# Moving the end of a scan chunk off VectorE, six convolution pairs to TensorE, and a looser queue in layer 0

## The chip, the cores and the metric

The kernel runs on one core of one Trainium2 chip, in one launch. The metric is the device time of that launch in microseconds (us), the median of several runs. Five engines work side by side, each through its own queue in order: TensorE (PE; its weight loads are PEld), VectorE (DVE), ScalarE (ACT), GpSimd (POOL) and SyncE (SP), which here issues only DMA transfers. They meet through semaphores. PE writes its results to PSUM tiles, which DVE and ACT read; the other tiles lie in SBUF.

## What is computed

Two layers on x of shape 4 x 256 x 512 (1024 tokens in 8 blocks of 128), each with a residual.

Layer 0 is an attention with 32 heads over latents of width 4, followed by a gated feed-forward of hidden width 1792:

```python
C_q = x @ Wq_d + bq_d ; C_kv = x @ Wkv_d + bkv_d
q = (C_q @ W_qk + b_qk).reshape(b, s, 32, 4)
attn = softmax(einsum('bqhd,bkd->bhqk', q, C_kv) / sqrt(4))
x = x + (attn over C_kv @ Wv_u + bv_u) @ Wo + bo + down(silu(gate(x)) * up(x))
```

Layer 1 is a selective-scan block (1024 channels, 16 states, a causal convolution of 4 taps) beside a feed-forward with a router that picks two of eight low-rank experts:

```python
x, z = split(hidden @ in_proj_w)
xc = silu(conv_b + sum over k of conv_w[:, k] * x shifted by 3 - k)
dt, Bm, Cm = rmsnorm'd parts of xc @ x_proj_w ; dt = softplus(dt @ dt_proj_w + dt_bias)
h_t = exp(dt_t * A) * h_(t-1) + dt_t * B_t * x_t        # for 1024 x 16 states, 256 steps
y = (sum over n of h * C + D * xc) * silu(z)
out = y @ out_proj_w
```

The four batches of 256 tokens are independent in the scan.

## The kernel before

**Layer 0** lets PE work without a break. The feed-forward is written as a generator, `gate_up` and then `down`, that issues a few matmuls at each step; `go(ff, n)` takes n steps of it. The attention's pieces are issued between such steps, so that PE has feed-forward matmuls in its queue while other engines finish the attention's evictions. Weights of gate and up (`wgu`, 256 KB each) are fetched by POOL's queue three tiles ahead.

Each batch first needs its latents (`latents`, L284 to L338, a generator as well, taken one `yield` at a time). It projects the keys and queries, copies them out of PSUM, and splits them into a rounded high part (ACT) and the rest as a low part (DVE's subtraction: `ks` on L296, `q` low on L320). L310 multiplies q out, DVE adds its bias and scales it (L314, twice), and four spread matmuls give `qg`, whose evictions on L337 alternate between DVE and ACT. `scores_max` (L352, L354) then has PE write scores into PSUM and DVE take their maxima, 64 reductions in all; PE reuses the two score banks once DVE is through with them. Two passes of `maxima` and `attention` cover the four batches. Before layer 1, SP loads the in-projection's weights `w_in`, 512 KB for a pair of chunks (L621): the first as soon as the pool is open, the second and third inside the loop over the last normalization (L633 to L636).

**Layer 1's scan** is a loop over u = 0 to 127 (4 batches x 8 chunks of 128 channels x 4 groups of four states). A step is, in this order of the queues: ACT computes four decays for step u + 2 (L958, 128 x 255 each); DVE multiplies `bx` (L964, 128 x 1024, into PSUM) from `brow` and `dus`; DVE runs the scan (L979); POOL multiplies the states by C into `hc` (L984); PE sums hc over the states into the PSUM tile `ysum` (L996, one step later). There are two h tiles, three hc tiles and one ysum. When the four steps of a chunk are through, `close_chunk` (L1000), issued two steps after the chunk's last, multiplies ysum with silu(z) and writes the chunk's result: on DVE, between bx and the scan. The next chunk's first matmul into ysum (L994) follows it.

All other work of a batch (the next batch's normalization, in-projection, convolution, step sizes dt, and the last batch's output and experts) is put into the loop by a table written out by hand: `put(b, s, f, ...)` runs f at step s of batch b, ahead of bx, and `put_late` at its end. `dt` and `du = dt * x` of a pair of chunks are stored to DRAM by SP (`send`) and read back in the scan's layout, `dts` and `dus` (`spread`, four transfers of 32 partitions each, two tiles deep). For batch 0 the table holds later steps than for the others, because its second half has to be made while its first half is scanned: `step_out` (three POOL operations that finish dt) and `step_x` (POOL's du).

The convolution takes two chunks, a pair, at a time: `conv_in` at one step and `conv_taps` at the next. From batch 1 on, the pair's first chunk is convolved by PE with four diagonal matrices that ACT scales (L767, L789) and evicted by ACT (L791); the second chunk is four scaled copies on ACT (L768 and L772) that POOL adds up (L795, three adds of 128 x 256).

## Time and profile before

The median of three runs is 850.35 us (850.3 to 854.58). One execution was profiled:

| | |
|---|---|
| profiled execution, whole | 852.26 us |
| its span in the trace | 850.5 us |
| mean granted clock of PE | 0.954 |
| busy: PE, DVE, ACT, POOL | 740.6, 669.6, 538.6, 489.1 us |
| DVE scan, L979 | 129 times, 2234 ns each |
| DVE bx, L964 | 128 times, 1232 ns |
| POOL hc, L984 | 130 times, 2322 ns |
| ACT decays, L958 | 504 times, 498 ns |
| DVE closing multiply, L1000 | 32 times, 416 ns, after 9.7 us of idle |
| POOL convolution adds, L795 | 45 times, 729 ns |

How to read it. A line of the timeline is: start, duration, engine, source line, operation, the tile written and those read, shapes, how many were joined; in brackets how long the engine had been idle before, and what ended that idle time. A line of the waits gives the same summed over the execution: engine and tile, what it waited for, and total us, times and the longest. The busy table says how long each engine worked, but not whether anybody waited for it; the granted clock says at what share of full speed PE was let run in a stretch.

### The profile page before, as it was taken

How to read it: one execution, taken by the hardware profiler on the slowest of the kernel's cores; microseconds unless marked ns; L12 is line 12 of the kernel's file. 1: busy time of each engine (PE TensorE's matmuls, PEld its weight loads, DVE VectorE, ACT ScalarE, POOL GpSimd, SP SyncE). 2: the span in 40 equal slices, each digit the busy share in tenths (PEclk: the TensorE clock that was granted, in tenths of full speed). 3: DMA queues.
4: the chain of work that ended last, by engine and by line, in shares of the span. 5: the costliest groups of instructions: out<-in, count | busy, mean ns of one | idle time of the engine just before them, and what ended most of it. 6: DMA issues, size and time to landing. Idle time of an engine off the chain costs nothing.

```text
span 850.5 us, 10982 instructions
## 1 busy us (share of the span) xinstructions
PE 740.6 (87%) x3798; PEld 423.6 (50%) x3798; DVE 669.6 (79%) x647; ACT 538.6 (63%) x1061; POOL 489.1 (58%) x376
## 2 busy tenths in 40 slices
PE   5999999989999899989778888887898997956875
PEld 3565546656555676656444346344356444312331
DVE  4597755478744435798799999899999999999996
ACT  4225565223566267599885789786888885855561
POOL 3223322001343333669967689869599759697664
PEclk9999999899999999999898999989999979998998
DMA  7234332001222322555751644433553343443400
GB/s 223 68 94 125 88 86 62 0 1 38 75 75 79 113 56 63 139 147 161 206 142 50 173 137 124 123 100 109 156 155 99 102 112 102 109 119 105 112 25 25
DMA packets 67202, 86.71 MB, mean 102 GB/s; under 512 B 12061, under 2 KB 52009, under 8 KB 66762
## 3 DMA queue, kind: packets, MB, share of 16 engines
q1 hardware_dynamic: 57786, 67.12, 28.5%
q0 software_dynamic: 9072, 18.35, 7.8%
q8 instruction: 30, 0.49, 0.2%
q10 hardware_dynamic: 288, 0.52, 0.2%
q14 instruction: 26, 0.21, 0.1%
HBM read 66.58 MB, written 10.22 MB: 90 GB/s over the span
## 4 chain that ended last, share of the span: by engine, by line
PE 37%; DVE 30%; POOL 12%; ACT 8%; issue 6%; DMA 4%; SPq 1%; DVEq 0%; POOLq 0%; ACTq 0%
DVE h L979 18%; POOL hc L984 7%; PE pu L444 6%; PE pg L444 6%; DVE bx L964 6%; ACT decay L958 4%; PE av L397 4%; PE po L469 3%; PE scT L386 2%; DVE mpl L354 2%; PE px L753 2%; POOL xc L795 2%; PE pz L926 2%; DMA dus<-dud 2%; PE ysum L996 1%
## 5 line engine op out<-in xcount | busy, mean ns | idle before, releaser
L984 POOL TENSOR_TENSOR hc<-h,cr 128x1024 f32<-128x1024 f32 (+1 forms) x130 | 301.6, 2322 | 96.4 <-DVE h L979 76.6
L979 DVE TENSOR_TENSOR_SCAN h<-decay,bx 128x1024 f32<-128x1024 f32 (+1 forms) x129 | 288.0, 2234 | 16.3 <-PE po L469 4.0
L958 ACT ACTIVATE decay<-dts,aneg 128x255 f32<-128x255 f32 x504 | 213.3, 498 | 97.5 <-DVE h L979 87.2
L964 DVE TENSOR_TENSOR bx<-brow,dus 128x1024 f32<-128x1024 f32 x128 | 157.7, 1232 | 8.7 <-DMA dus<-dud 4.6
L996 PE MATMUL ysum<-hc,stack 128*32 128x256 f32 x1024 | 88.1, 413 | 60.1 <-POOL hc L984 59.8
L456 POOL TENSOR_TENSOR hlo<-g,hhi 128x512 fp32r<-128x512 f32 x28 | 35.9, 1281 | 118.3 <-ACT hhi L455 118.3
L427 POOL DMA_DIRECT2D wgu<-in_wgu x56 | 31.2, 558 | 97.3 <-PE pg L444 95.9
L354 DVE TENSOR_REDUCE mpl<-sc 128x4 f32<-128x1024 f32 x64 | 76.4, 1217 | 12.4 <-PE sc L352 12.2
L996 PEld LDWEIGHTS ysum<-hc,stack 128*32 128x32 f32 x1024 | 21.2, 111 | 120.7 <-POOL hc L984 98.1
L388 ACT ACTIVATE pe<-scT 128x1024 f32<-128x1024 f32 x64 | 64.0, 1023 | 23.4 <-PE sc L352 16.8
L1088 PE MATMUL po<-ow,xc 128*128 128x512 f32 x128 | 70.4, 659 | 2.2 <-DVE xc L1000 2.2
L926 PE MATMUL pz<-xn1T,w_in 128*128 128x256 f32 x256 | 67.5, 411 | 0.0
L753 PE MATMUL px<-xn1T,w_in 128*128 128x256 f32 x256 | 61.8, 387 | 0.1
L926 PEld LDWEIGHTS pz<-xn1T,w_in 128*128 128x128 f32 x256 | 49.0, 200 | 19.0 <-issue 10.8
L753 PEld LDWEIGHTS px<-xn1T,w_in 128*128 128x128 f32 x256 | 48.2, 192 | 13.1 <-issue 4.3
L452 DVE SCALAR_TENSOR_TENSOR g<-g,pg 128x512 f32<-128x512 f32 x28 | 19.2, 686 | 41.5 <-ACT g L451 41.5
L444 PE MATMUL pu<-xhi,wgu 128*128 128x512 f32 x112 | 48.7, 435 | 2.3 <-DMA wgu<-in_wgu 2.3
L469 PE MATMUL po<-wd,hhi 128*128 128x512 f32 x112 | 50.3, 449 | 0.0
L444 PE MATMUL pg<-xhi,wgu 128*128 128x512 f32 x112 | 48.9, 437 | 0.0
L455 ACT CAST hhi<-g 128x512 fp32r<-128x512 f32 x28 | 17.3, 619 | 48.5 <-DVE g L454 48.5
L444 PE MATMUL pu<-xlo,wgu 128*128 128x512 f32 x112 | 45.4, 405 | 0.0
L469 PE MATMUL po<-wd,hlo 128*128 128x512 f32 x112 | 45.0, 401 | 0.0
(230 smaller groups left out, 1251.7 us busy)
## 6 DMA issues: line engine op xcount, KB each, us to landing
dts<-dtd SPq DMA_DIRECT2D x124, 128.0 KB, 2.9
dus<-dud SPq DMA_DIRECT2D x124, 128.0 KB, 3.0
wgu<-in_wgu POOLq DMA_DIRECT2D x56, 256.0 KB, 2.8
w_in<-in_inx SPq DMA_DIRECT2D x16, 512.0 KB, 4.3
w_in<-in_inz SPq DMA_DIRECT2D x16, 512.0 KB, 4.9
dtd<-dt SPq DMA_DIRECT2D x15, 256.0 KB, 2.2
dud<-du SPq DMA_DIRECT2D x15, 256.0 KB, 2.2
wd<-in_wd POOLq DMA_DIRECT2D x7, 512.0 KB, 3.6
```

The lines of the kernel that those rows point to most:

```text
L354: nc.vector.tensor_reduce(mpl2[b % 2][:, qb, 2 * hp : 2 * hp + 2, 16 + 2 * gq : 18 + 2 * gq], sc.rearrange("p i (f k) -> p i f k", f=2), A ...
L388: nc.scalar.activation(pes[b, k][:, 2 * t : 2 * t + 2, :], sc, AF.Exp)
L444: mm(ps, lhsT=wgus[i][:, hc, :], rhs=xs[j][:, hc, :], start=(hc == 0 and j == 0), stop=(hc == HC - 1 and j == 1))
L469: mm(po, lhsT=hids[th][j][:, m, i * P : (i + 1) * P], rhs=wd[:, m, :], start=False, stop=(m == MC - 1 and j == 1))
L753: mm(px[:, i, :], lhsT=w[:, i, hc, :], rhs=xns[b][:, hc, :], start=(hc == 0), stop=(hc == HC - 1))
L926: mm(pz[:, i, :], lhsT=w[:, i, hc, :], rhs=xns[b][:, hc, :], start=(hc == 0), stop=(hc == HC - 1))
L958: nc.scalar.activation(da[:, k, 1:], live["dts", b, c][:, k, 1:], AF.Exp, scale=aneg[:, c, k, g : g + 1])
L964: nc.vector.tensor_tensor(bx, brow[g // 2][:, g % 2, :].unsqueeze(1).to_broadcast([P, NG, S]), live["dus", b, c], ALU.mult)
L979: nc.vector.tensor_tensor_scan(h[:, n].rearrange("p n t -> p (n t)"), da[:, n].rearrange("p n t -> p (n t)"), bx[:, n].rearrange("p n t -> ...
L984: (nc.vector if k == NG - 1 else nc.gpsimd).tensor_tensor(hc[:, n], h[:, n], crows[b][:, g, :].unsqueeze(1).to_broadcast([P, NG // parts, ...
L996: mm(ysum[k * NB : (k + 1) * NB, :], lhsT=stack, rhs=hc[:, k, :], start=False, stop=(g == NU - 1))
L1088: mm(live["po", b, i], lhsT=xcs[b][:, c, i * P : (i + 1) * P], rhs=late_w["ow"][:, c, :], start=False, stop=(c == DC - 1))
```

## The change

In `latents`, both low-part subtractions are issued one step of the generator later; the two q evictions go from DVE to ACT, with a bias that is scaled beforehand (`bhalf`); all four qg evictions go to ACT.

The second and third w_in loads go from SP's queue to ACT's, and from inside the last normalization's loop to behind it.

`close_chunk` is parted. `take_sum` copies ysum to the chunk's place, on ACT at the head of the step, ahead of the decays (the first chunk on DVE where L1000 was). `gate` multiplies the copy with silu(z) on POOL, behind the step's hc. The last chunk is closed on DVE as before.

For six pairs (`both`) the second chunk is convolved by PE too: four diagonals into the space of the tap tile instead of the four scaled copies, four matmuls, one eviction on ACT, and no adds on POOL.

For batch 0, the table's steps for step_out, step_x and the spreads from chunk 4 on change.

```diff
-        nc.vector.tensor_tensor(ks[32:40, :], kT, ks[0:8, :].bitcast(F32), ALU.subtract)
         cq = ap1.tile([P, 512], F32, tag="rd", name="cq")[:QL, 0:S]
         nc.scalar.activation(cq, pl[:QL, 0, :], AF.Identity, bias=wqk[:, 0:1])
         yield
+        nc.vector.tensor_tensor(ks[32:40, :], kT, ks[0:8, :].bitcast(F32), ALU.subtract)
         yield
...
-            nc.vector.tensor_scalar(
-                q8[:, hf, :], pq[:, hf, :], blat[:, hf : hf + 1], 1.0 / KVL**0.5,
-                ALU.add, ALU.mult,
-            )
+            nc.scalar.activation(q8[:, hf, :], pq[:, hf, :], AF.Identity,
+                                 bias=bhalf[:, hf : hf + 1], scale=1.0 / KVL**0.5)
         part = [ap1.tile([P, 2, S], F32R, tag=f"q{n}", name=f"q{n}") for n in ("hi", "lo")]
         nc.scalar.copy(part[0], q8)
+        yield
         nc.vector.tensor_tensor(part[1], q8, part[0].bitcast(F32), ALU.subtract)
-        yield
...
-            (nc.scalar.copy if gq % 2 else nc.vector.tensor_copy)(qg[:, gq], p)
+            nc.scalar.copy(qg[:, gq], p)
...
-    for i, _ in enumerate(norm):
+    for _ in norm:
         go(ff, 2)
-        if i in (1, 3):
-            w_of["x", 0, i // 2 + 1] = weights(inx_d, i + 1)
-    go(ff)
+    for p in (1, 2):
+        w_of["x", 0, p] = weights(inx_d, 2 * p, nc.scalar)
+        go(ff, 4 if p == 1 else 1000)
...
+    both = ((1, 0), (1, 3), (2, 1), (2, 3), (3, 1), (3, 3))
...
+        if (b, p) in both:
+            tp = tp.rearrange("p k t -> p (k t)")
+            for k in range(KC):
+                nc.scalar.activation(tp[:, k * P : (k + 1) * P], ident, AF.Identity,
+                                     scale=v[1][:, V_CW + k : V_CW + k + 1])
+        else:
...
+        if (b, p) in both:
+            dg = live["tap"].rearrange("p k t -> p (k t)")
+            for k in range(KC):
+                mm(px[:, 1, :], lhsT=dg[:, k * P : (k + 1) * P], rhs=pads[p % 2][:, 1, k : k + S],
+                   start=(k == 0), stop=(k == KC - 1))
+            nc.scalar.activation(xc, px[:, 1, :], AF.Identity, bias=vec[:, c + 1, V_CB : V_CB + 1])
+        else:
...
-    def close_chunk(b, c):
-        nc.vector.tensor_tensor(
-            xcs[b][:, c, :], ysum, szs[b, c // 2][:, c % 2, :], ALU.mult
+    def take_sum(b, c):
+        (nc.scalar.copy if b or c else nc.vector.tensor_copy)(xcs[b][:, c, :], ysum)
+
+    def gate(b, c):
+        nc.gpsimd.tensor_tensor(
+            xcs[b][:, c, :], xcs[b][:, c, :], szs[b, c // 2][:, c % 2, :], ALU.mult
         )
...
-        for q, us in enumerate(((5, 6, 7), (10, 12, 14)) if b else ((8, 9, 11), (15, 17, 18))):
+        for q, us in enumerate(((5, 6, 7), (10, 12, 14)) if b else ((9, 10, 11), (13, 15, 16))):
...
-        for p, u in ((2, 8 if b else 13), (3, 16 if b else 19)):
+        for p, u in ((2, 8 if b else 11), (3, 16 if b else 17)):
...
-            o = 0 if b or c < 4 else 2
+            o = 0 if b or c < 4 else 1
...
+        last = u - 2
+        shut = (last // PER, last % PER // NU) if last >= 0 and last % NU == NU - 1 else None
+        if shut and shut != (0, 0) and u < total:
+            take_sum(*shut)
         if 3 <= u < total - 2:
             decays(u + 2)
...
-        last = u - 2
-        if last >= 0 and last % NU == NU - 1:
-            c = last % PER // NU
-            close_chunk(last // PER, c)
-            if last // PER == B - 1:
-                late.append(c)
+        if shut == (0, 0):
+            take_sum(0, 0)
+        if u > total:
+            b, c = shut
+            nc.vector.tensor_tensor(xcs[b][:, c, :], ysum, szs[b, c // 2][:, c % 2, :], ALU.mult)
         if u < total:
             scan(u, 1 if u < total - 1 else 4)
...
+        if shut and u < total:
+            gate(*shut)
...
+        if shut and shut[0] == B - 1:
+            late.append(shut[1])
```

More of the change, by code (lines that the diff above doesn't have):

```diff
@@ L136, in block_kernel @@
     mask = ap1.tile([P, 8], F32, name="mask")
+    bhalf = ap1.tile([P, 2], F32, name="bhalf")
     zk = ap1.tile([P, NTB, 56], F32, name="zk")
@@ L171, in masks @@
         nc.vector.tensor_scalar_mul(mask, mask, -1.0)
+        nc.vector.tensor_scalar_mul(bhalf, blat[:, 0:2], 1.0 / KVL**0.5)
     def fold_load():
@@ L617, in block_kernel, with weights @@
     we = ctx.enter_context(tc.tile_pool(name="we", bufs=1, side="right"))
-    def weights(d, c0):
+    def weights(d, c0, eng=nc.sync):
         t = we.tile([P, 2, HC, P], F32, tag="w_in", name="w_in", bufs=3)
-        nc.sync.dma_start(t, d[:, c0 : c0 + 2])
+        eng.dma_start(t, d[:, c0 : c0 + 2])
         return t
@@ L767, in conv_in @@
                 nc.scalar.activation(dg[:, k, :], ident, AF.Identity, scale=v[0][:, V_CW + k : V_CW + k + 1])
-        nc.scalar.activation(xcs[b][:, 2 * p + 1, :], px[:, 1, :], AF.Identity,
-                             bias=v[1][:, V_CB : V_CB + 1], scale=v[1][:, V_CW + KC - 1 : V_CW + KC])
-        tp = w1.tile([P, KC - 1, S], F32, tag="tap", name="tap")
-        for k in range(KC - 1):
-            nc.scalar.activation(tp[:, k, :], pads[p % 2][:, 1, k : k + S], AF.Identity,
-                                 scale=v[1][:, V_CW + k : V_CW + k + 1])
-        live["tap"] = tp
+        tp = live["tap"] = w1.tile([P, KC - 1, S], F32, tag="tap", name="tap")
+        if (b, p) in both:
[4 more added lines that the diff above has]
+        else:
+            nc.scalar.activation(xcs[b][:, 2 * p + 1, :], px[:, 1, :], AF.Identity,
+                                 bias=v[1][:, V_CB : V_CB + 1], scale=v[1][:, V_CW + KC - 1 : V_CW + KC])
+            for k in range(KC - 1):
+                nc.scalar.activation(tp[:, k, :], pads[p % 2][:, 1, k : k + S], AF.Identity,
+                                     scale=v[1][:, V_CW + k : V_CW + k + 1])
         if b == 0:
@@ L793, in conv_taps @@
         xc = xcs[b][:, c + 1, :]
-        for k in range(KC - 1):
-            nc.gpsimd.tensor_tensor(xc, xc, live["tap"][:, k, :], ALU.add)
+        if (b, p) in both:
[5 more added lines that the diff above has]
+        else:
+            for k in range(KC - 1):
+                nc.gpsimd.tensor_tensor(xc, xc, live["tap"][:, k, :], ALU.add)
     def conv_silu(b, z=None):
```

## The prediction

> **What bounds the kernel now.** I read the page's busy table first, then its chain, then the waits, then the timeline wherever the bounding engine paused.
>
> ```profile
> PE 740.6 (87%) x3798; PEld 423.6 (50%) x3798; DVE 669.6 (79%) x647; ACT 538.6 (63%) x1061; POOL 489.1 (58%) x376
> ...
> DVE h L979 18%; POOL hc L984 7%; PE pu L444 6%; PE pg L444 6%; DVE bx L964 6%; ACT decay L958 4%; PE av L397 4%; PE po L469 3%; PE scT L386 2%; DVE mpl L354 2%; PE px L753 2%; POOL xc L795 2%; PE pz L926 2%; DMA dus<-dud 2%; PE ysum L996 1%
> ```
>
> No engine binds throughout. The slices show two regimes. Up to 355.5 us (layer 0 and the entry to layer 1) PE has nine tenths nearly everywhere. From there to 842 us DVE has nine tenths; its step is bx (1.23), a bubble of about 0.13, the scan (2.29) and 0.04, together 3.69 us, 128 times. So a gain must be a PE pause before 355 or a DVE pause after it. The loop's timeline of DVE shows the pauses:
>
> ```profile
> 360.74 0.43 DVE L1000 TENSOR_TENSOR xc<-ysum,sz 128x256 f32<-128x256 f32 x1 [1.18 <-ACT sz L932]
> ...
> 376.83 0.42 DVE L1000 TENSOR_TENSOR xc<-ysum,sz 128x256 f32<-128x256 f32 x1 [1.17 <-PE ysum L996]
> 377.17 2.28 DVE L979 TENSOR_TENSOR_SCAN h<-decay,bx 128x1024 f32<-128x1024 f32 x1
> 379.48 1.23 DVE L964 TENSOR_TENSOR bx<-brow,dus 128x1024 f32<-128x1024 f32 x1
> ...
> 394.64 0.43 DVE L1000 TENSOR_TENSOR xc<-ysum,sz 128x256 f32<-128x256 f32 x1 [2.87 <-PE ysum L996]
> ...
> 407.78 1.23 DVE L964 TENSOR_TENSOR bx<-brow,dus 128x1024 f32<-128x1024 f32 x1 [3.18 <-DMA dus<-dud]
> ```
>
> The closing multiply L1000 stands between a step's bx and its scan. Where its sum or its gate is late, the scan waits for an operation it does not need. The waits view puts the totals at 8.5 (L1000 on ysum, six times), 1.2 (on sz) and 4.6 (bx on the dus transfer, twice).
>
> **Layer 0.** Two PE pauses in the second maxima pass:
>
> ```profile
> 174.01 0.50 PE L352 MATMUL sc<-km,qg 32*128 32x256 f32 x4 [0.72 <-DVE mpl L354]
> 175.14 0.50 PE L352 MATMUL sc<-km,qg 32*128 32x256 f32 x4 [0.63 <-DVE mpl L354]
> ```
>
> PE waits for reductions that free its score banks, and DVE is late because it stood 2.57 us on ACT's copy ahead of L296 at 172.28 while reductions were ready behind it. The change issues L296's subtraction one piece later, so this idle goes. Per latents, DVE also loses two q evictions (L314, 0.48 each) and two qg evictions (L337, 0.69 each): 2.3 us. The same kind of pause stands at 38.26 (0.42), 52.46 (0.63), 186.52 (1.04), 187.65 (0.63) and 195.76 (0.40). From 188 to 192 the granted clock is 0.57, after the pair before it: 4 x 0.43 = 1.7 us of lost clock. All of it together is 0.42 + 0.63 + 1.35 + 1.67 + 1.7 + 0.40 = 6.2. ACT takes on two 0.47 evictions (row L791, same source and size) and two qg copies of 0.59 per latents, 2.1 us each and 8.4 in all. Its qg copies now wait 19.6 us for PE, and that hides them; were PE to wait for every one, 8.4 would be lost. Ends: 8.4 lost, 6.2 gained. I take **4.7**, near the gain, because the late engine in these rows is DVE; a quarter is left for pauses that return behind another reduction.
>
> **The w_in loads.** Two 512 KB loads go from SP, where they were issued at 278.9 just ahead of the last wgu load, to ACT's queue behind the tanh and the cast of the last hidden tile (286.8 and 292.3 now).
>
> ```profile
> 284.55 0.40 PE L444 MATMUL pg<-xlo,wgu 128*128 128x512 f32 x1
> 287.26 0.77 PE L444 MATMUL pu<-xhi,wgu 128*128 128x512 f32 x1 [2.31 <-DMA wgu<-in_wgu]
> ```
>
> The wgu load took 5.9 us where the median is 2.8, with DMA at 0.98 in this stretch; alone it lands near 284.0. PE does not get all of the 2.31: the next stop, L464, needs the last o8n, which DVE writes at 288.70 to 288.99 (now L464 starts at 290.74). Gain 290.74 - 288.99 = 1.75, plus a little clock: **2.0**, ends 0.5 and 2.3. The moved loads take 4.3 us each and their px readers start after 298: hidden by the pair in front. Uncovered, they would cost a few us.
>
> One rule bears on both parts. The clock after the idle 2.31 is 0.51 for 3.4 us (287.3 to 290.7). The Trainium skill ("TensorE: Matmul & The Clock Gate", section on HAM oscillation) says that only idle gaps beyond about 3.4 us cool the clock; by it this slow stretch has another cause and stays, and layer 0 would give 3.0 instead of 4.7. The row, a shorter gap followed by the slow clock, decides.
>
> PE stays the bound to 355.5, where the loop's first scan waits for its last `down` matmul, so these 6.7 us pass through whole.
>
> **Closing a chunk.** DVE loses L1000 31 times. The multiply fills the bubble between bx and scan, so it does not cost its 0.42: a closing step measures 3.79 and the next 3.67, 0.08 over two plain ones, x31 = **2.5**. The larger part is the waits: 1.18 at step 5 (the new copy on DVE needs no sz; **1.1**), 1.17 and 2.87 at steps 9 and 13, and 1.82, 0.53 and 1.39 at steps 49, 57 and 81 (**3.7**).
>
> ACT gets a 128x256 copy at the head of every fourth step (0.47 by L791), ahead of the four decays of step u+2. If the sum is late ACT waits, and behind it stand those decays, for which the scan would wait. By the timeline a sum whose last hc is two steps old is there before ACT reaches the place in all but a few steps (0.6 us late at worst), and the decays end 2.8 to 8 us before their scan. Cost nothing; uncovered, see the third rival.
>
> POOL gets 31 multiplies of 128x256, nearest row L795, 0.73 each: 22.6 us. The convolution takes 6 x 3 of those same adds off it: 13.1. Net 9.5, on a POOL that is busy 404 of the loop's 508 us and waits 77 for the scan. The Trainium skill ("GPSIMD Engine Reference", section on engine selection) advises against GpSimd for two-input elementwise work, about twice VectorE's time. hc against bx on the same shape agrees (2.35 against 1.23), and by engine time alone 31 x 0.31 = 9.6 us would be lost. But DVE binds here and POOL does not, on average.
>
> **Six pairs by TensorE.** Each adds what L789 does now for a pair's other chunk, 8 PE instructions; L789's 96 instructions take 24.6 us for 12 chunks, 2.05 each: 12 in all. On ACT, xc and three taps (0.47 + 3 x 0.50) become four diagonals of 0.29 spaced and an eviction of 0.47: even. PE waits 59.8 us for hc in the loop, which hides its share; the eviction waits for PE as L791 does now (5.4 in four waits), inside the decays' lead. Cost nothing. Uncovered, 12 us.
>
> **The schedule of batch 0.** The du products (step_x) of pairs 2 and 3 and the second step_out come two steps earlier, the first step_out one later, the spreads from chunk 4 on one earlier. Step 16 waited 3.18 for a chain in which the du product came at step 13, its store was issued at 397.99 and landed 5.4 later, and the spread was issued at 403.41. Two steps (7.4 us) earlier it is in time. Step 20 waited 1.43 on a spread that now comes one step (3.69) earlier, but behind the store of pair 3 on SP, which waits for POOL: 0.3 stays. With 1.17 and 2.87 of steps 9 and 13, 3.18 + 1.43 - 0.3 + 4.04 = 8.3 go. What is late next is POOL. From step 9 to 16 it gets eight hc (2.33 spaced), seven 128x512 operations (1.25) and eight of 128x256 (0.73): 18.6 + 8.8 + 5.8 = 33.2 in 8 x 3.69 = 29.5 us of DVE. It starts about 2.1 late, because step_out's first operation waits for ACT's e (2.25 at 375.46 now). With two h buffers hc may start 3.69 + 1.40 - 2.33 = 2.76 late before a scan waits: 3.7 + 2.1 - 2.76 = 3.0 come back, as scans waiting for hc around steps 14 to 18. Net **5.3**.
>
> **The sum.** 4.7 + 2.0 + 1.1 + 2.5 + 3.7 + 5.3 = 19.3. The profiled execution took 852.26 (span 850.5 and 1.8 around it), 1.9 above the median of the runs: 833.0 against it, 831.0 against the median. Forecast **832**, between them. All gains in full, 6.2 + 2.3 + 1.2 + 2.9 + 3.9 + 8.6 = 25.1, give 825; the low ends (layer 0 nothing, w_in 0.5, batch 0 half) give 840.
>
> **Rivals.** *POOL takes DVE's place.* The gates delay hc wherever POOL has a backlog. All of batch 0 and the 3.7 come back as scans waiting for hc: gains of 4.7 + 2.0 + 1.1 + 2.5 = 10.3 stay, time 841. For it: POOL works without a pause from 375 to 396 now. Against it: at steps 43 and 47 two tap groups (2.2 each) leave.
>
> *Layer 0's pauses move.* The reductions are slower than PE anyway, and the next one waits: layer 0 gives nothing, 14.6 remain, 836.5. For it: DVE is 83% busy from 176 to 186. Against it: the 2.57 us idle.
>
> *ACT's queue binds (slower).* take_sum waits for ysum at ACT's head, decays and then scans start late, hc and the next sum with them. It decides where the sum is later than the decays' lead of 2.8. If it is one step late (3.69 + 0.47) at each of 31 closes, 1.36 x 31 = 42 are lost and 19.3 gained: 874. From 3.4 late on the kernel is slower (2.8 + 19.3/31). Against it: no sum in the timeline is that late.
>
> *Nothing much moves*: PE's pauses return and the waits only change names: 850.
>
> **Chances.** Forecast 0.60, POOL 0.14, layer 0 0.13, ACT 0.07, nothing 0.06. A measurement tells 0.5% (4.3 us) from no change. Faster 0.87, same 0.06, slower 0.07. The range goes from 824 to 843.
>
> **What would show it.** Right: no DVE wait over 0.3 at steps 5, 49, 57 and 81; closing steps at 3.69; bx without a DMA wait; POOL's gate near 0.73; PE without pauses near 174 and 285; some waits of h for hc around step 16. Wrong: h waiting for decay after a copy of ysum (ACT), h waiting for hc at every close (POOL), or the first loop scan less than 4 us earlier (layer 0).

## The result, and the profile after

The changed kernel takes 849.59 us, the median of 20 runs (848.95 to 857.65), against 853.62 for the kernel before in its 20 (846.16 to 856.52). The ratio of the kernels over these runs is 0.9986 with a 95% interval of 0.9963 to 1.0009 (the two medians alone give 0.9953): no change that can be told, where 832 was forecast. Executions of one kernel differ with TensorE's granted clock: of those of before, all under 848 us had a mean of 0.953 to 0.962, and all over 856 one of 0.936 to 0.946. The profiled execution took 849.32 us, its span 847.5, against 850.5.

The span hides two large and opposite differences, which the starts of two scans in each timeline of VectorE part. I use them throughout: the **entry** is the start of step 4's scan, where layer 0 ends for VectorE, and the **stretch** is the time from there to the scan of step 127.

| | before | changed |
|---|---|---|
| entry | 355.55 | 346.92 |
| stretch | 484.74 | 490.37 |
| rest | 10.2 | 10.2 |

In these two traces the entry is 8.6 us earlier, where 6.7 was forecast. The stretch is 5.6 longer, where 12.6 shorter was forecast. The page of the changed kernel shows the chain away from VectorE (its share was 30%, that of ScalarE 8%, of TensorE 37%):

```profile
PE 748.9 (88%) x3846; PEld 428.7 (51%) x3846; DVE 654.5 (77%) x602; ACT 554.7 (65%) x1113; POOL 496.6 (59%) x389
...
PE 50%; DVE 16%; ACT 14%; POOL 12%; issue 4%; DMA 3%; SPq 1%; ACTq 0%; DVEq 0%; POOLq 0%
DVE h L996 9%; POOL hc L1001 8%; ACT decay L975 6%; PE pg L444 6%; PE pu L444 5%; PE po L469 5%; PE av L397 4%; PE po L1109 4%; PE px L755 3%; PE ysum L1013 3%; PE scT L386 2%; PE pp L826 2%; DVE mpl L354 2%; PE pz L943 2%; DMA dus<-dud 2%
```

VectorE does 15 us less and PE, ScalarE and GpSimd 8, 16 and 7.5 more. That VectorE worked less and finished no earlier says that it waits. Its waits inside the loop (the waits view from 326 to 839 us: total, times, longest):

```profile
DVE bx L981 <- DMA dus<-dud: 5.4, 1, 5.4
DVE m L1056 <- ACT ml L1034: 5.2, 2, 3.1
DVE h L996 <- POOL hc L1001: 4.5, 3, 2.9
DVE h L996 <- ACT decay L975: 4.2, 3, 2.0
...
DVE nrm L840 <- ACT rs L711: 3.3, 2, 2.2
```

None of these names stood among the loop's waits of before except the first. The line left out is the wait for layer 0's last matmuls at the entry, 4.0 before. The sum is 22.6 us. What stood in their place before were the waits of steps 9, 13, 16, 20, 49, 57 and 81 (12.4). All are gone as forecast but one: step 16's is 5.42 instead of 3.18 and is the first line above. Most of step 5's went too (0.8), and the closing steps measure 3.69 instead of 3.79 (with the step behind each, 0.70 over the eight closes from step 94 to 126, so some 2.7 in all). 22.6 - 12.4 - 0.8 - 2.7 = 6.7, of the size of the 5.6 by which the stretch grew. So what the change was to remove was removed, but for step 16, and somewhat more came in.

### The profile page after: what moved, and what is told of

It reads as the page before. It is cut to its first block, busy times and chain, and to the rows that moved or that the text cites. A ratio compares the mean times of both kernels' runs of the same rounds, so it can differ in the third digit from the quotient of the medians.

```text
span 847.5 us, 11090 instructions
## 1 busy us (share of the span) xinstructions
PE 748.9 (88%) x3846; PEld 428.7 (51%) x3846; DVE 654.5 (77%) x602; ACT 554.7 (65%) x1113; POOL 496.6 (59%) x389
## 4 chain that ended last, share of the span: by engine, by line
PE 50%; DVE 16%; ACT 14%; POOL 12%; issue 4%; DMA 3%; SPq 1%; ACTq 0%; DVEq 0%; POOLq 0%
DVE h L996 9%; POOL hc L1001 8%; ACT decay L975 6%; PE pg L444 6%; PE pu L444 5%; PE po L469 5%; PE av L397 4%; PE po L1109 4%; PE px L755 3%; PE ysum L1013 3%; PE scT L386 2%; PE pp L826 2%; DVE mpl L354 2%; PE pz L943 2%; DMA dus<-dud 2%
## 5 line engine op out<-in xcount | busy, mean ns | idle before, releaser
L975 ACT ACTIVATE decay<-dts,aneg 128x255 f32<-128x255 f32 x504 | 214.5, 503 | 58.9 <-DVE h L996 48.5
L456 POOL TENSOR_TENSOR hlo<-g,hhi 128x512 fp32r<-128x512 f32 x28 | 35.8, 1280 | 117.1 <-ACT hhi L455 117.1
L943 PE MATMUL pz<-xn1T,w_in 128*128 128x256 f32 x256 | 71.8, 430 | 0.0
L943 PEld LDWEIGHTS pz<-xn1T,w_in 128*128 128x128 f32 x256 | 51.8, 212 | 21.1 <-issue 12.3
L444 PE MATMUL pg<-xlo,wgu 128*128 128x512 f32 x112 | 44.1, 393 | 0.0
```

The costliest lines, as they stand in the source:

```text
L444: mm(ps, lhsT=wgus[i][:, hc, :], rhs=xs[j][:, hc, :], start=(hc == 0 and j == 0), stop=(hc == HC - 1 and j == 1))
L943: mm(pz[:, i, :], lhsT=w[:, i, hc, :], rhs=xns[b][:, hc, :], start=(hc == 0), stop=(hc == HC - 1))
L975: nc.scalar.activation(da[:, k, 1:], live["dts", b, c][:, k, 1:], AF.Exp, scale=aneg[:, c, k, g : g + 1])
```

## The experiments

Five theories are told apart. A: the six pairs make ScalarE late. B: the copy of the sum at ScalarE's head does. C: the transfer of step 16 is late because of weight loads beside it. D and E, formed after the first two rounds: behind the mends it is ScalarE's own queue (D) or TensorE's (E) that holds back the norm and the router.

Each kernel is the changed one with the edit shown, unless it says otherwise. Medians in us, ratio to the kernel before on the same chip with its interval, entry and stretch from one trace each. The kernels ran on several chips, where the medians of before were 851.6 to 854.6; so a difference of some 3 us between two medians shows little by itself, and two ratios are told apart where their intervals do not meet. The changed kernel's is 0.9963 to 1.0009.

| kernel | median | ratio, interval | entry | stretch |
|---|---|---|---|---|
| layer0_only | 844.72 | 0.993, 0.9888 to 0.9971 | 346.7 | 487.3 |
| w_in_only | 854.72 | 1.0021, 0.9987 to 1.0054 | 353.7 | 488.8 |
| no_both | 845.93 | 0.9938, 0.9901 to 0.9975 | 348.7 | 489.9 |
| no_p3 | 844.72 | 0.9939, 0.9905 to 0.9974 | 348.6 | 489.2 |
| close_on_dve | 851.87 | 1.0014, 0.9983 to 1.0044 | 345.6 | 494.3 |
| sum_behind | 858.46 | 1.0078, 1.0047 to 1.0109 | 346.7 | 500.7 |
| old_table | 853.67 | 0.9991, 0.9957 to 1.0025 | 347.1 | 490.8 |
| groups_first | 844.74 | 0.9913, 0.9883 to 0.9942 | 345.6 | 485.9 |
| loads_later | 848.26 | 0.9967, 0.9933 to 1.0001 | 345.4 | 489.3 |
| groups_loads | 844.59 | 0.9913, 0.9886 to 0.9941 | 345.5 | 486.2 |
| groups_loads_route | 845.06 | 0.9935, 0.990 to 0.997 | 346.5 | 485.9 |
| five_pairs | 846.56 | 0.992, 0.9888 to 0.9951 | 347.1 | 484.9 |
| act_relief | 844.75 | 0.9922, 0.9894 to 0.9951 | 347.5 | 486.2 |
| pe_relief | 845.35 | 0.9926, 0.9888 to 0.9964 | 348.3 | 485.9 |
| pz_behind | 841.64 | 0.987, 0.9808 to 0.9931 | 348.7 | 488.4 |
| pz_behind_loads | 837.45 | 0.9828, 0.978 to 0.9876 | 346.9 | 478.6 |
| before_again | 851.79 | 0.9989, 0.9948 to 1.003 | 353.6 | 482.3 |
| after_again | 849.06 | 0.9971, 0.9934 to 1.0007 | 348.5 | 494.2 |

### How much is a draw

**before_again, after_again**: the two kernels unchanged.

> The kernel before, profiled a second time. The one trace of before has 484.7 us from the scan of step 4 to that of step 127; the same loop behind the changed layer 0 had 487.3 and behind the moved loads 488.8. If the loop's time is one of the code, this run has 484 to 485.5; if it depends on how the transfers and the clock fall in an execution, it lies anywhere from 484 to 490.

> The changed kernel, profiled a second time: its loop had 490.4 us from step 4 to step 127. The waits on ScalarE at steps 51, 83 and 86 (1.8, 2.0 and 3.1) are of the code and come again within 0.5; the one of step 16 (5.4) belongs to the transfers and may differ by 2.

Before: 482.3 instead of 484.7, outside the narrow expectation; with layer0_only and w_in_only the same loop code has 482.3 to 488.8. After: 494.2 instead of 490.4; the waits of steps 51, 83 and 86 came again to 0.01 us (1.78, 1.97, 3.07), step 16's was 5.16, and 2.9 of new waits for decays came at steps 12 and 13. So the loop differs by several us from trace to trace: in the changed kernel before step 22 alone, in the old loop there, at step 57 and once at 86. The means are 485.8 (four traces) and 492.3 (two): by these the change lengthens the loop by some 6, not only in one trace. The entry is a draw as well: 353.57 in before_again and 348.53 in after_again, so 5 to 9 us earlier, 6.8 between the means.

What differs ahead of step 22 can be read in the traces. From 12.5 to 20 us behind the entry (steps 7 to 9) TensorE's granted clock is 0.58 or 0.59 in after_again, no_both, no_p3, pz_behind and w_in_only, and 1.00 in the other fifteen traces. In all twenty a pause of TensorE of 1.92 to 1.94 us (L737 or L739) comes 7.3 us behind the entry, and a clock of 0.50 follows it; by windows of 1 us it lasts about 3.4 us in the changed kernel's first trace and about 10 in after_again. The same matmuls there, in the first trace and in after_again:

```profile
359.75 1.99 PE L755 MATMUL px<-xn1T,w_in 128*128 128x256 f32 x8
```

```profile
362.62 3.78 PE L755 MATMUL px<-xn1T,w_in 128*128 128x256 f32 x8
...
373.42 0.37 ACT L1018 COPY xc<-ysum 128x256 f32<-128x256 f32 x1 [2.39 <-PE ysum L1013]
...
379.90 2.29 DVE L996 TENSOR_TENSOR_SCAN h<-decay,bx 128x1024 f32<-128x1024 f32 x1 [0.86 <-ACT decay L975]
385.53 2.29 DVE L996 TENSOR_TENSOR_SCAN h<-decay,bx 128x1024 f32<-128x1024 f32 x1 [2.08 <-ACT decay L975]
```

TensorE is late with the sum of the close at step 9, ScalarE's copy waits for it (not at all in the first trace), and the decays of steps 12 and 13 behind it are late. At step 25 after_again is 3.9 us behind the first trace (99.98 against 96.10 from the entry); from there to step 127 the two take 394.2 and 394.3. So the stretches of these five traces compare with those of the others only to within some 4 us. Why the half clock lasts longer in some executions is not shown.

### Layer 0

**layer0_only**: the kernel before with the edits of `latents`, `bhalf` and the w_in loads. **w_in_only**: before with the loads alone.

> The kernel before with the change's layer 0 part and its w_in loads alone. Theory A says these parts kept what was forecast (6.7 us) and the scan lost the rest: the loop's first scan starts 7 to 9 us earlier than before, the scan's own waits stay those of before (steps 9, 13, 16, 20, 49, 57, 81), and the time is 6 to 9 us below before, so below the whole change. Rival: layer 0's gain is taken back at the loop's entry or by the next transfer, and the time is within 3 us of before.

> The kernel before with the two moved w_in loads alone. The forecast gave them 2.0 us: the last wgu load lands before its matmul needs it, so the pause of 2.31 at 285 goes and L464 starts 4.2 to 4.5 us after the last pg matmul instead of 6.2; the time falls by 1 to 3 us. Rival: the pause stays above 1.5 since another wait takes its place, and the time is within 1 us of before.

layer0_only holds the theory: its entry is that of the whole change, and with the old loop it is 4.9 us faster than the whole change by the medians (the intervals of the ratios still meet, 0.9888 to 0.9971 and 0.9963 to 1.0009). w_in_only's entry is 1.9 us earlier than in the first trace of before, which looks like the 2.0 forecast, but it is not earlier than before_again's (353.69 against 353.57), and its median is that of before. Its trace of PE at the place:

```profile
284.56 0.40 PE L444 MATMUL pg<-xlo,wgu 128*128 128x512 f32 x1
285.71 0.50 PE L444 MATMUL pu<-xhi,wgu 128*128 128x512 f32 x1 [0.76 <-DVE g L454]
...
288.85 1.52 PE L464 MATMUL po<-m_att,o8n 128*128 128x512 f32 x3 [1.00 <-DVE rd L413]
```

The pause for wgu is gone, a shorter one for VectorE stands there, and L464 starts where the last reciprocal lets it, 1.89 earlier than before. The granted clock behind the pause is 1.00 instead of 0.51. In before_again, without the edit, the pause is there and the clock behind it is 1.00 too (286.9 to 290.3):

```profile
284.10 0.40 PE L444 MATMUL pg<-xlo,wgu 128*128 128x512 f32 x1
286.87 0.47 PE L444 MATMUL pu<-xhi,wgu 128*128 128x512 f32 x1 [2.37 <-DMA wgu<-in_wgu]
288.79 1.88 PE L464 MATMUL po<-m_att,o8n 128*128 128x512 f32 x4
```

From the start of the last pg matmul to that of L464 it is 6.19 us in before, 4.69 in before_again and 4.29 in w_in_only. So 1.5 of the 1.9 was the half clock of one execution, and the moved loads by themselves took off 0.4. The other 7.0 us of layer0_only's entry (353.7 to 346.7) belong to the edits of `latents`.

### One part undone at a time

**no_both**: `both = ()`. **no_p3**: `both = ((1, 0), (2, 1), (3, 1))`.

> The changed kernel without the six pairs: GpSimd adds up every pair's second chunk as before. The forecast held the pairs to cost nothing and to relieve GpSimd; by it this kernel is 2 to 6 us slower than the changed one, with scans waiting for hc. Theory A: the waits for decays at 51 and 83 and for the norm at 53 go, GpSimd's waits of steps 12 to 18, 49 and 81 appear instead, and the time is 0 to 5 us below the changed kernel.

> The changed kernel, but only the first of the two pairs of each batch is convolved whole by TensorE (three pairs instead of six); the last pair of a batch is added up by GpSimd as before. Theory A: the last pair is the one that ends ahead of the silu, the norm and the router on ScalarE, so the scan's waits for decays at steps 51 and 83, for the norm at 53 and for the router's logits at 22 and 86 fall to half or less (they are 12.7 us in all); GpSimd gets 3 x 2.4 us more, of which 0 to 4 come back as scans waiting for hc. Net 3 to 8 us faster than the changed kernel. Theory B: those waits stay within 0.5 us each and the time gets longer by GpSimd's share.

By the medians the six pairs cost 3.7 us (849.59 against 845.93), and the three last ones alone 4.9; the forecast had nothing. The intervals of the ratios just meet the changed kernel's, so by themselves these runs do not settle it. In both traces the waits at 51, 53 and 83 are gone and scans wait for hc instead (12.7 us in no_both), as theory A said; the traces' stretches are only 0.5 and 1.2 shorter, but both are among the five with the long half clock, which cost after_again 3.9.

**close_on_dve**:

```diff
-        if shut and shut != (0, 0) and u < total:
-            take_sum(*shut)
...
-        if shut == (0, 0):
-            take_sum(0, 0)
-        if u > total:
+        if shut:
             b, c = shut
             nc.vector.tensor_tensor(xcs[b][:, c, :], ysum, szs[b, c // 2][:, c % 2, :], ALU.mult)
...
-        if shut and u < total:
-            gate(*shut)
```

> The changed kernel, but every chunk is closed by VectorE's multiply between bx and the scan, as before; no copy on ScalarE and no multiply on GpSimd. The forecast gave the parting of the close 7.3 us and more: by it this kernel is 5 to 10 us slower than the changed one. Theory A (ScalarE's lead is what the change used up; copies of 11 us and their 18 us of waiting for sums are part of it): the decays' waits at 51 and 83 shrink below 1, VectorE waits for sums at 3 to 6 closes instead, and the time is within 4 us of the changed kernel.

2.3 us slower by the medians, with intervals that overlap, and 3.9 by the stretch: the parting of the close is worth about that, not the 7.3 of the forecast. VectorE waits for sums at ten closes, 15.3 us, and ScalarE's lead is back (it waits 83.2 us for scans, against 48.5); no scan waits above 0.3 for decays at steps 51 and 83 any more.

**sum_behind**:

```diff
-        if shut and shut != (0, 0) and u < total:
-            take_sum(*shut)
         if 3 <= u < total - 2:
             decays(u + 2)
+        if shut and shut != (0, 0) and u < total:
+            take_sum(*shut)
```

> The changed kernel, but ScalarE's copy of the sum is issued behind the decays of the step, not ahead of them. Theory B: ScalarE's copies wait 18 us for the sums in the scan; taken behind the decays, the scan's waits for decays at steps 51 and 83 (1.8 and 2.0) go and the time falls by 3 to 6 us. Theory A: the decays come 0.4 us earlier at closing steps, steps 51 and 83 change by less than 0.6, and the time stays within 1.5 us; TensorE starts the next chunk's sums 1.7 us later, which costs nothing or gives GpSimd's hc some waits.

Both theories missed it: 9 us slower. The waits view shows who pays for 1.7 us more of delay at each close:

```profile
PE ysum L1011 <- ACT xc L1018: 23.2, 14, 3.2
POOL xc L1021 <- ACT xc L1018: 13.0, 5, 5.4
```

In the changed kernel these were 4.2 and 5.4. TensorE cannot start the next chunk in the one ysum tile before the copy, and all its queue stands behind; GpSimd's gate stands ahead of the next hc. Of the two places tried for the copy, the head of ScalarE's queue is the better one. Theory B falls for steps 51 and 83, where the waits grew to 2.50 and 2.68.

**old_table**: the three lines of the table for batch 0 as before.

> The changed kernel with the table of before for batch 0 (step_out, step_x and spreads at their old steps). Theory C (the new steps put the stores and the spread of step 16 among the weight loads of steps 11 to 15, and the old ones among those of 13 and 15): bx waits 2 to 4 us at step 16 and 0 to 2 at step 20, GpSimd's wait of step 14 shrinks, and the time is within 2 us of the changed kernel; by the forecast it would be 4 to 5 us slower.

The median is 4 us higher with runs from 847.8 to 856.0, but the ratio is that of the changed kernel (0.9991 against 0.9986) and the stretch only 0.5 longer: no difference is shown in the time. bx waits 7.4 at step 16 and 2.1 at step 20. So the new steps did shorten the chain; the transfer was late all the same.

### Mends

**groups_first**:

```diff
                 mm(px[:, 0, :], lhsT=live["dg"][:, k, :], rhs=pads[p % 2][:, 0, k : k + S],
                    start=(k == 0), stop=(k == KC - 1))
+            if (b, p) in both:
+                dg = live["tap"].rearrange("p k t -> p (k t)")
+                for k in range(KC):
+                    mm(px[:, 1, :], lhsT=dg[:, k * P : (k + 1) * P], rhs=pads[p % 2][:, 1, k : k + S],
+                       start=(k == 0), stop=(k == KC - 1))
             nc.scalar.activation(xcs[b][:, c, :], px[:, 0, :], AF.Identity,
                                  bias=vec[:, c, V_CB : V_CB + 1])
...
-            dg = live["tap"].rearrange("p k t -> p (k t)")
-            for k in range(KC):
-                mm(px[:, 1, :], lhsT=dg[:, k * P : (k + 1) * P], rhs=pads[p % 2][:, 1, k : k + S],
-                   start=(k == 0), stop=(k == KC - 1))
```

> The changed kernel, but in a pair that TensorE convolves whole, the second group of four matmuls is issued ahead of the eviction of the first. Theory A (the pairs make ScalarE late): in the changed kernel the second group (L807) waits 5.1 us for the first eviction and the second eviction (L809) waits 12.5 us for it, 2.1 a pair. Both waits then go or are joined into one of about 2 us or less, the scan's waits for the decays at steps 51 and 83 (1.8 and 2.0) shrink by 0.4 to 2 each, and the time falls by 2 to 6 us. Theory B (the copy of the sum at ScalarE's head makes the decays late): steps 51 and 83 stay as they are, within 0.3, and the time within 1.5 us.

Theory A holds: 4.9 us faster by the medians, with intervals that do not meet, and 4.5 by the stretch. The reason can be read in the changed kernel's timeline, TensorE at a pair of batch 1, then ScalarE at the last pair of batch 2:

```profile
376.21 1.99 PE L807 MATMUL px<-pad,tap 128*128 128x256 f32 x8 [2.02 <-ACT xc L801]
```

```profile
530.78 0.48 ACT L801 ACTIVATE xc<-px,vec 128x256 f32<-128x256 f32 x1 [1.93 <-PE px L799]
533.34 0.48 ACT L809 ACTIVATE xc<-px,vec 128x256 f32<-128x256 f32 x1 [2.08 <-PE px L807]
533.72 1.70 ACT L975 ACTIVATE decay<-dts,aneg 128x255 f32<-128x255 f32 x4
```

The second group writes the other half of the same PSUM tile, and waits until ScalarE has evicted the first half; ScalarE then waits for the second group, 2.08 us in each of six pairs (12.5), and behind it stand the four decays, the silu and the norm. With both groups issued first, ScalarE waits once and evicts twice. That one wait is longer, so its waits at the evictions fall from 16.7 us to 12.2, not to nothing (the trace of groups_first, at the same step):

```profile
527.06 0.47 ACT L806 ACTIVATE xc<-px,vec 128x256 f32<-128x256 f32 x1 [3.36 <-PE px L804]
527.43 0.47 ACT L810 ACTIVATE xc<-px,vec 128x256 f32<-128x256 f32 x1
527.79 1.69 ACT L976 ACTIVATE decay<-dts,aneg 128x255 f32<-128x255 f32 x4
```

The waits of steps 51 and 83 fall from 1.77 and 1.97 to 0.52 and 0.67, that of step 14 for hc from 2.85 to 0.87, and the norm's of step 21 (2.17) goes; step 16's grows to 6.46. The order was the pairs' price as far as it can be told: with the edit they are 1.2 better than no pairs, which is within the noise.

**loads_later**:

```diff
-                put(b, 9 + 2 * k, load_late, n)
+                put(b, (9, 18, 20, 22)[k], load_late, n)
```

> The changed kernel, but three weight loads of layer 1's second half (1 MB, 0.25 MB and 2 MB) are issued at steps 18, 20 and 22 of the scan instead of 11, 13 and 15. Theory C (the dus transfer of step 16 lands late because it shares the DMA engines with these loads): bx of step 16 waits 0 to 2 us instead of 5.4, and the time falls by 3 to 5, unless ScalarE's or GpSimd's lateness around steps 14 to 22 takes it back. Rival: the transfer was late because its own chain (GpSimd's products, the store, SP's order) is late; then the wait stays above 4 us.

Theory C holds for the wait (1.27 instead of 5.42), and not for the time. VectorE in the changed kernel, then in this one, at step 16:

```profile
391.28 2.29 DVE L996 TENSOR_TENSOR_SCAN h<-decay,bx 128x1024 f32<-128x1024 f32 x1
398.99 1.23 DVE L981 TENSOR_TENSOR bx<-brow,dus 128x1024 f32<-128x1024 f32 x1 [5.42 <-DMA dus<-dud]
```

```profile
393.20 1.23 DVE L981 TENSOR_TENSOR bx<-brow,dus 128x1024 f32<-128x1024 f32 x1 [1.27 <-DMA dus<-dud]
396.41 2.29 DVE L996 TENSOR_TENSOR_SCAN h<-decay,bx 128x1024 f32<-128x1024 f32 x1 [1.97 <-POOL hc L1001]
```

SP's queue in the changed kernel, then in this one, shows why:

```profile
380.34 0.43 SPq L1227 DMA_DIRECT2D bw<-in_base  x1
380.88 0.38 SPq L928 DMA_DIRECT2D dtd<-dt  x1
...
387.88 1.75 SPq L934 DMA_DIRECT2D dts<-dtd  x4
...
390.67 1.80 SPq L934 DMA_DIRECT2D dus<-dud  x4
```

```profile
378.78 0.38 SPq L928 DMA_DIRECT2D dtd<-dt  x1
...
383.45 1.75 SPq L934 DMA_DIRECT2D dts<-dtd  x4
...
385.78 1.79 SPq L934 DMA_DIRECT2D dus<-dud  x4
```

The larger part is the store ahead of the spread. In the changed kernel the store of dt was issued 0.5 us behind the 1 MB load `bw` and took 6.95 us to land, where stores of its kind take 2.4 in the median; without that load it took 4.6, and the spread of step 16 was issued 3.4 us earlier, counted from the entry. The spread itself, between a load of 0.25 MB and one of 2 MB in the changed kernel, took 6.9 us to land (3.1 in the median over the execution), without them 5.9. With the loads moved, waits for hc at step 16 (1.97) and for the decays of step 20 (2.10) come in and take most of it back; the norm's at step 21 is hardly smaller (1.67 instead of 2.17). It is 1.3 us by the medians, which the intervals do not tell from nothing, and 1.1 by the stretch.

**groups_loads**: both edits. **groups_loads_route**: also `put(b, 23, route_exp, b)` for 22. **five_pairs**: also without the pair (2, 3).

> The changed kernel with both mends: the second group of matmuls ahead of the first eviction, and the three weight loads at steps 18, 20 and 22. Theories A and C together: the scan's stretch from step 4 to step 127 (484.7 us before, 490.4 in the changed kernel, 485.9 with the groups alone, 489.3 with the loads alone) comes to 481 to 484, because bx of step 16 waits under 2 us and the waits behind it that the loads alone met (hc at 16, decays at 20, norm at 21) are ScalarE's and shrink with the groups. The time is 839 to 844. Rival: the step 16 wait only moves on to hc and the decays again, and the stretch stays at 485 to 486.

> As the kernel with both mends, and VectorE's first router operations (route_exp) one step later, at 23 of a batch instead of 22, since at steps 22 and 86 they wait 1.4 and 3.2 us for ScalarE's copies of the logits while the scan stands behind them. If the lateness is one of order on VectorE alone, both waits go, the stretch from step 4 to 127 falls by another 3 to 4.6 us and the time to 836 to 841. Rival: ScalarE's next operation is late by as much, and the scan waits for decays or the norm instead; then less than 1.5 us is won.

> As the kernel with both mends and the later router step, but without the last pair of the second batch's convolution among those on TensorE (five pairs). Theory A: the waits of steps 51 (0.5) and 53 (1.1) go; GpSimd, which gets 2.4 us at step 47, makes no scan wait more than 0.5. The time falls by 0.5 to 1.6 us. Rival: GpSimd's adds delay hc as they did in batch 3 with three pairs (2.6 us at steps 79 to 81), and the time rises by 0.5 to 2.5.

All three stay at groups_first's time. The rival held for the first (3.4 us ahead at step 17, 0.7 at step 22). For the second the wait at 86 (3.17) went, and one of 5.65 on ScalarE's ex came at step 89 in VectorE's next router operation. For the third the wait at 51 went (0.5; that at 53 had gone with the later router step), and the stretch is 0.9 shorter, but the median is not better.

### Whose queue is late

**act_relief**, on groups_first: for b of 2 and 3, `range(KC if b == 1 else 1)` and `range(KC if b == 1 else 0)` for the diagonals of L772 and L777, so most diagonals of batches 2 and 3 are left out (the first group's diagonals then lie in one fixed tile, which the second group of these batches reads too). **pe_relief**, on groups_first: `for hc in range(HC if b < 1 else 1)` in pz_mm, which leaves out three quarters of the z projection of batches 1 to 3.

> The kernel with the groups first, and for batches 2 and 3 most of ScalarE's diagonals left out (20 operations of 0.3 us a batch, some 6 us; the convolution of these batches then uses stale or wrong weights, the same matmuls run). Theory D: ScalarE's own queue is what is late ahead of the norm and the router. Then the scan's waits at steps 51, 53, 83, 85 and 86 (0.5, 1.1, 0.7, 1.4, 3.2 with the groups first) fall to less than half in sum, batch 1's (steps 14 to 22) stay, and the time falls by 3 to 6 us. Rival E: TensorE's queue is what is late and ScalarE waits for it; then ScalarE's waits for TensorE grow by what was left out and the sum stays above 5.

> The kernel with the groups first, and for batches 1 to 3 three quarters of the z projection left out on TensorE (1.5 us of each half pair, 12 us a batch; the gate is then wrong). Theory D: the waits at 51, 53, 83, 85 and 86 stay above 5 us in sum and the time within 2 us. Rival E: they fall to less than half, and the time falls by 3 to 6.

Theory D falls: with less work on ScalarE the waits at 51, 53, 83, 85 and 86 are 0.5, 0, 2.9, 0 and 3.1, 6.5 in sum against 6.9. With less on TensorE they are 0, 0, 0, 0 and 2.5. Rival E held, except for the time: new waits for decays (0.7, 2.0, 1.9 at steps 38, 70, 102) took the place. They go with the granted clock, whose mean is 0.913 in this trace and 0.951 in groups_first: over steps 32 to 36, 64 to 68 and 96 to 100 it is 0.88, 0.81 and 0.77, against 1.00, 1.00 and 0.88. Over all twenty traces, a wait above 0.3 at step 38 or 70 stands only where the clock of these four steps was 0.90 or less, and every such trace has one. So leaving work out of TensorE's queue did not leave the rest as it was, and this kernel's time says nothing against E.

**pz_behind**, on groups_first:

```diff
-        for p, at_i, at_g in ((2, (14, 15), 16), (3, (22, 24), 25)):
+        for p, at_i, at_g in ((2, (14, 15 if nxt == B else 16 if b else 17), 16), (3, (22, 24), 25)):
```

**pz_behind_loads**: the same with the loads later.

> The kernel with the groups first, and the second half of the z projection's third pair, 2.0 us of TensorE, issued behind the last convolution pair of the next batch instead of ahead of it (batches 0 to 2). Theory E: with the z matmuls cut the waits of steps 51, 53, 83 and 85 (0.5, 1.1, 0.7, 1.4 with the groups first) went to 0; moved behind, they fall to under 1.5 in sum without leaving work out, and the stretch from step 4 to step 127 (485.9) falls by 2 to 3.5 us. Rival: ScalarE then waits for these matmuls at the silu of the gate, which stands right behind the convolution's silu, and the waits stay above 2.5 in sum.

> As the kernel with the z matmuls moved behind, and the three weight loads at steps 18, 20 and 22. The mended transfer of step 16 won 3.4 us up to step 17 and lost them by step 22 to the norm, the spread of step 20 and the router. Theory E: part of that second loss was TensorE's queue too, so at step 25 the lead against the kernel without the loads' move stays at 1.5 us or more, and the stretch comes to 480 to 483. Rival: the chain of batch 1's norm is held by something else; the lead at step 25 is under 1 us.

The order is enough: in pz_behind the waits at 51, 53 and 85 are 0 and that at 83 is 0.4. Its median is 3.1 below groups_first, from four runs of 839.8 to 849.1 whose interval overlaps that of groups_first; its one trace is among the five with the long half clock, with waits at steps 12 to 16 (0.9, 2.5 and 6.4) as after_again had, and one of 1.3 at step 38, so the stretch of 488.4 does not show the gain. With the loads moved too, 837.45 with four runs within 0.5, faster than both kernels. The clean comparison is with groups_loads, which differs by this edit alone: 7.1 us by the medians, with intervals that do not meet (0.978 to 0.9876 and 0.9886 to 0.9941), and 7.6 by the stretch. What VectorE waits for in its loop:

```profile
DVE m L1057 <- ACT ml L1035: 3.9, 2, 2.1
DVE h L997 <- PE po L469: 3.6, 1, 3.6
DVE h L997 <- POOL hc L1002: 3.6, 3, 2.1
DVE bx L982 <- DMA dus<-dud: 1.6, 2, 1.1
DVE h L997 <- ACT decay L976: 1.0, 2, 0.5
DVE xc L1372 <- PE ysum L1014: 1.0, 1, 1.0
DVE nrm L841 <- ACT rs L711: 0.6, 1, 0.6
```

Without the entry's wait (po) and the tail's (L1372) these are 10.7 us, where the changed kernel had 22.6. From entry to step 25 it takes 90.6 us, groups_first 92.8 and groups_loads 92.2: more of the gain of the moved loads is kept once TensorE's queue is in order. The stretch is 478.6, 11.7 below the changed kernel's.

## Why the prediction was wrong

*Layer 0 and w_in* (4.7 + 2.0): the sum of 6.7 held (8.6 in the profiled pair, 5.0 in the second, 6.8 between the means), its parts did not. The edits of `latents` gave 7.0. The loads gave 0.4, not 2.0: the 1.75 was read from a start of L464 that the half clock of that one execution had made 1.5 late. Nor did the row decide about the clock. A pause of 2.31 was followed by 0.51 in before, one of 2.37 at the same place by 1.00 in before_again; the pauses of 1.04 and 0.63 at 186 to 188 were followed by 0.57, 0.60 and 0.57 in before, before_again and w_in_only, and the one of 1.9 at the loop's entry by 0.50 in every trace. So half clock did follow pauses shorter than the 3.4 us that the prediction names, but not each of them, and the measured rows decide against reading that figure as a bound.

*Closing a chunk* (2.5 + 1.1 + 3.7): what it removed was removed, some 2.7, 0.8 and 3.7. "Cost nothing" for ScalarE's copy was wrong in kind. The copies are 11.0 us of work and wait 18.2 for sums; ScalarE's waiting for scans, which was its spare time, fell from 87.2 to 48.5. In the profiled execution no single copy made a scan wait; the lead that hid the other edits was used up (close_on_dve, which gives it back, has no waits at 51 and 83). In after_again one copy did: it waited 2.39 for its sum at step 9's close, and the scans of steps 12 and 13 waited 2.9. Undone alone, the part proves worth 2 to 4 us, not clear of the noise.

*Six pairs by TensorE*: this is the step that failed first. It said "even" for ScalarE, "PE waits 59.8 us for hc in the loop, which hides its share", and "inside the decays' lead". The operations were counted rightly and the two waits between them were not: a second group that waits for the first eviction, and a second eviction that waits for the second group, 2.1 us a pair, at the place where TensorE's queue has the z projection in front and ScalarE's has the decays, the silu and the norm behind. An idle time summed over 508 us hid nothing at steps 45 to 53. Measured: 3.7 us by undoing it, 4.9 by mending the order, and only the second is clear of the noise.

*The schedule of batch 0* (5.3): "Two steps (7.4 us) earlier it is in time" failed. It took the store's 5.4 us and the spread's 3 from the trace and moved them, and did not look at what else the DMA queues would then carry. The spread was issued 4.1 us earlier against the entry, not 7.4, and took 6.9 to land. The wait of step 16 was 5.42 instead of none. The trace of before had the warning: there too the 1 MB load stood right ahead of the store of dt (387.63 and 388.48), which took 6.7. The POOL term has the right number by luck: 2.85 us of waiting for hc at step 14, 3.0 forecast from a backlog of GpSimd's own work. There was no backlog; GpSimd stood idle for ScalarE's scaled copies just ahead of that hc,

```profile
382.90 2.35 POOL L812 TENSOR_TENSOR xc<-xc,tap 128x256 f32<-128x256 f32 x3 [2.52 <-ACT tap L783]
```

and with the groups first, which brings ScalarE there earlier, this idle is 0.52 and the wait of step 14 is 0.87.

*The sum.* The forecast took each removed wait as a gain. groups_loads shows why it is not: removing step 16's wait let VectorE run up against the norm and the router of the next batch. TensorE's queue sets part of these: with it in order (pz_behind_loads) the norm's wait at step 21 is 0.60 instead of 1.67, the router's at step 22 stays at 2.08. The waits of before were partly hidden slack of those chains. The rival "ACT's queue binds" named the engine that VectorE came to wait for, but not the main cause (it blamed the copy, which did it at one close of after_again), and the rival "POOL takes DVE's place" did not occur. Of the 17.6 us between the forecast and the measured time, 12.1 came back, by the medians, by changing only when the same operations are issued (pz_behind_loads).

What stays open: why the half clock behind the same pause lasts three times as long in some executions, and what holds the 5.5 us between pz_behind_loads and the forecast.

## What to carry to other kernels

Ahead of moving work to engines that look idle, follow the next two chains that end at the same place (here the next batch's projection, convolution, norm and router) and count what they have to spare at that very step, not over the loop. Two groups of matmuls into one PSUM tile with an eviction between them cost two handovers; issue both groups, then both evictions. Before a transfer is moved earlier, look at which large loads stand ahead of it and of its store (here 1 MB, and the store took 6.95 us instead of 2.4). Mends add up only when the chain behind each is mended too (here 4.9, 3.1 and, alone, 1.3 us by the medians, and 12.1 together). And ahead of reading a gain of 2 us from one trace, look at the granted clock of the stretch in a second one.

## What the runs showed of the hardware

In these traces a VectorE operation with two inputs in SBUF stood still while a GpSimd operation that began before it ran. The router's ex, 0.19 us in both places of before, in layer0_only (VectorE, then GpSimd):

```profile
673.14 2.34 DVE L1038 TENSOR_TENSOR ex<-ml,m 128x32 f32<-128x32 f32 x1
```

```profile
673.07 2.36 POOL L986 TENSOR_TENSOR hc<-h,cr 128x1024 f32<-128x1024 f32 x1 [1.67 <-DVE h L981]
```

It ends at 675.48, 0.05 after hc. So do those of 1.45 us in w_in_only, of 1.97 and 1.10 in close_on_dve and of 0.90 in groups_first, each begun behind an hc and ended 0.04 or 0.05 after it. In before, where the same operation began at 682.06, ahead of hc at 682.09, it took 0.19. L414 takes 1.25 to 1.28 instead of 0.29 wherever a low-part subtraction of GpSimd (L456) began 0.16 ahead of it, four times of sixteen in each trace that was read for it. The scan and bx, which read one input from PSUM, keep 2.29 and 1.23 beside hc. The Trainium skill ("SBUF — State Buffer", section "SBUF: two separate sides") states such a lock between VectorE with two SBUF inputs and GpSimd, held by the one that starts first for its whole instruction; these rows agree.
